# Two vision state-space layers on one core: output stages interleaved with the next batch's norm and projection, the second layer's preparation as a pipeline

## The chip, the core and the metric

The kernel runs on one core of one Trainium2 chip, as one program. The metric is the device time of one execution, in microseconds. The core has five engines that run side by side, each through its own queue in order: PE (TensorE, matmuls and transposes; it accumulates in PSUM), DVE (VectorE), ACT (ScalarE), POOL (GpSimd) and SP, which issues most of the DMA transfers. A few DMAs, the accumulating ones, are issued by POOL. PE's clock is throttled, and the profile shows what share of it was granted.

## The reference

Input x has 4 batches of 64 x 64 positions with 192 channels, float32. Two layers follow. The first is a selective scan in four directions. Cut to what matters (`xs` are the four orders of the positions; a group norm stands ahead of the projection and a residual is added behind):

```python
xz = jnp.einsum('bhwc,ec->bhwe', x, in_proj_weight)
xin, z = jnp.split(xz, 2, axis=-1)            # 384 inner channels each
xs = four orders of xin                       # rows, columns, both reversed
x_dbl = jnp.einsum('bkdl,kcd->bkcl', xs, x_proj_weight)
dts, Bs, Cs = split(x_dbl)                    # 12 + 16 + 16 rows
delta = softplus(dts @ dt_projs_weight + bias)
h = exp(delta * A) * h + delta * B * u        # along 4096 positions, 16 states
y_k = sum_n(h * C) + u * D
y = sum of the four directions, in place
out = (layernorm(y) * silu(z)) @ out_proj_weight.T
```

The second layer has the same outline. It has a 3 x 3 depthwise convolution with silu ahead of the scan, and its scan divides by a decay that falls below 1e-12 after few positions:

```python
decay = jnp.exp(jnp.cumsum(dt * A, axis=1))
h = decay * jnp.cumsum(dB_u / (decay + 1e-12), axis=1)
y = einsum(h, C) + u * D
```

## The kernel before, in words

A block is 512 positions (`LC`), so a batch has 8 (`NCH`); the 384 inner channels are 3 groups of 128 partitions (`ND`). A block in the layout "positions on partitions" is 4 tiles of 128 positions (`NJ`).

**First layer** (`FirstLayer.run`, once for each batch, one after the other):
- `norm` loads the 8 blocks of x (`xl`, three buffers), transposes them on PE into `xT`, takes statistics on DVE, and folds the result into the weights `w_in` and a bias, through a chain of small operations with a Sqrt on ACT.
- `project` (L500 on) runs over the 8 blocks: 6 matmuls to `pp`, evacuated by ACT to `u` (L522); 12 transposes to `q` (L529), copied by ACT to `ut` (L532) and multiplied by the sum of the D weights on DVE to `du` (L533). One DMA each stores `ut` and `du` (768 KB) to DRAM, into `uT` and into `y`, which starts with the D term. 6 more matmuls (L540) make the rows of dt, B and C by rows and by columns.
- `scans` keeps all engines but SP in an order written out by hand. It adds its results to `y` in DRAM, and leaves the gate z there too. The change doesn't touch it, except that it is told which y to use.
- `finish` is the output stage. `start` loads all 8 blocks of y (`yt`) and of the gate (`zg`, with a Silu on ACT, L873), in turn, and takes the mean and variance of each position (L881, L882): for the first two blocks, then for the other six, with one Sqrt (L884) for each of the two groups. `gated` scales `yt` on ACT (L896), transposes it on PE (L901), evacuates on ACT (L904) and multiplies by the gate on DVE (L907). `out` does the matmuls to `op` (L917), adds the input `xl` (L920) and stores. `gated` of the next block is written ahead of `out` of this one.

All four batches share one `y` in DRAM. The pools of `finish` and `project` reuse the same on-chip memory and PSUM banks, and one stage opens them after the other has closed them.

**Second layer** (`SecondLayer`), where each stage runs over all four batches:
- `project`: norm, projection, convolution; it leaves the positions near the borders in `uc`. Each direction's scan starts at a border and dies out within 256 positions, so only these are scanned.
- `prepare` has 8 steps (4 batches, the main 128 positions of each direction and an extension). A step loads `uc`, makes the dt, B and C rows (`xd`), and computes softplus: Abs (L1167) and Exp (L1168) on ACT, four operations on POOL (L1171 to L1175) with a Ln on ACT (L1174) beside them. On DVE follow the sum (L1177) and the running sums (line 989, a helper), the test whether the scan really died out (L1203 to L1206), and the product with u (L1241). PE transposes that, ACT copies it (L1222), and everything goes to DRAM (`keep`).
- `scans` has 9 scan steps for a batch, 36 in all, in an order written out by hand for PE, ACT, DVE and POOL: 4 of the main chunk with one state each, 2 of half chunks with two states, one of the extension, 2 of quarter chunks with four states. In each, ACT makes a weight (`sg`) and a decay (`a`); for the quarter chunks POOL multiplies ahead (L1285) and ACT does one wide activation (L1291). PE transposes the input (L1337), DVE weighs it (L1344) and scans, POOL multiplies by C (`c_product`, L1360), and PE adds it, transposed, to the outputs two steps later (L1378). The outputs of an extension (`yte`) and of the rest of a batch (`ytm`) are added to y in DRAM by 6 accumulating DMAs each, which POOL issues in a row (`store`, L1412 and L1415).
- `finish` is inherited and runs over all 32 blocks; the statistics of the next batch are started at the fifth block of this one.

Outside the two `scans` the order on each engine is made by the framework's scheduler at build time, from the order in which the program is written and from when it thinks operands are ready. A tile's memory is given out again when its readers are done; the number of buffers of each pool sets how far a producer can run ahead.

## Time and profile before

| | us |
|---|---|
| median of 3 runs | 11277.36 |
| lowest and highest | 11272.01, 11278.86 |
| the profiled execution, its own time | 11280.24 |
| its span, first to last instruction | 11278.4 |

| busy in the span | us | share |
|---|---|---|
| PE | 9593.1 | 85% |
| DVE | 9659.2 | 86% |
| ACT | 9787.2 | 87% |
| POOL | 8583.8 | 76% |

The mean granted clock of PE was 0.932. The stages, read from the first and last start of their lines in the trace (us from the span's start):

| stage | from | to |
|---|---|---|
| first layer, batch 0: norm and projection, start-up | 0 | 187.7 |
| its scans | 187.7 | 2397 |
| its output stage | 2397 | 2484 |
| batch 1: norm | 2484 | 2518 |
| projection | 2518 | 2608 |
| start-up of the scans | 2608 | 2657 |
| ... the same for the batches 1 to 3; last output stage | 9801 | 9886 |
| second layer: norm, projection, convolution | 9893 | 10456 |
| preparation | 10454 | 10648 |
| scans, with their start-up | 10648 | 11015 |
| output stage | 11015 | 11271 |

How to read the profile's lines. In a line of groups or waits, `L1177` is a line of the kernel and `dt<-dp,e` is what is written from what. A wait line says which engine at which line waited for which engine and line: us in total, how often, and the longest. A timeline line begins with the start and the length in us; in brackets stands how long the engine was idle ahead of it and what ended that. In a table by stretches, each engine has its busy time and the number of its instructions; PEclk is the granted share of PE's clock, then the busy share of the DMA engines and GB/s. In the strips of 40 slices each digit is a busy share in tenths.

### The profile page before, as it was taken

How to read it: one execution, taken by the hardware profiler on the slowest of the kernel's cores; microseconds unless marked ns; L12 is line 12 of the kernel's file. 1: busy time of each engine (PE TensorE's matmuls, PEld its weight loads, DVE VectorE, ACT ScalarE, POOL GpSimd, SP SyncE). 2: the span in 40 equal slices, each digit the busy share in tenths (PEclk: the TensorE clock that was granted, in tenths of full speed). 3: DMA queues.
4: the chain of work that ended last, by engine and by line, in shares of the span. 5: the costliest groups of instructions: out<-in, count | busy, mean ns of one | idle time of the engine just before them, and what ended most of it. 6: DMA issues, size and time to landing. Idle time of an engine off the chain costs nothing. (4 is left out here: it accounts for less than half of the span.)

```text
span 11278.4 us, 171696 instructions
## 1 busy us (share of the span) xinstructions
PE 9593.1 (85%) x61449; PEld 7301.6 (65%) x61449; DVE 9659.2 (86%) x11524; ACT 9787.2 (87%) x16986; POOL 8583.8 (76%) x2776
## 2 busy tenths in 40 slices
PE   7998888878988888888988888879988888788667
PEld 4776666655776666656766666647766666655356
DVE  4999899976999899957999899939998999888465
ACT  5999999977999999958999999949999999856567
POOL 3999899945999899928999899909998999700360
PEclk8999999988999999988999999979999999989688
DMA  4333333444333333344333334343333333434448
GB/s 124 109 105 98 94 98 100 97 133 125 109 104 99 94 99 98 97 149 112 111 100 96 96 98 98 89 164 107 109 100 94 98 98 98 127 114 128 159 104 272
DMA packets 831026, 1269.85 MB, mean 113 GB/s; under 512 B 99002, under 2 KB 514631, under 8 KB 829652
## 3 DMA queue, kind: packets, MB, share of 16 engines
q1 hardware_dynamic: 825300, 1252.49, 39.6%
q0 software_dynamic: 4864, 6.29, 0.4%
q8 instruction: 488, 8.00, 0.3%
q14 instruction: 374, 3.06, 0.1%
HBM read 958.19 MB, written 300.42 MB: 112 GB/s over the span
## 5 line engine op out<-in xcount | busy, mean ns | idle before, releaser
L738 POOL TENSOR_TENSOR h<-h,bct 128x1536 f32<-128x1536 f32 x2048 | 7062.4, 3469 | 591.4 <-DVE carry L734 487.9
L724 DVE TENSOR_TENSOR_SCAN h<-a,carry,x 128x512 f32<-128x512 f32 x5376 | 6607.0, 1267 | 238.7 <-PE x L716 191.7
L716 PE MATMUL x<-ident,xT 128*128 128x128 f32 x24576 | 4002.0, 287 | 817.7 <-DVE h L724 715.7
L699 ACT ACTIVATE xT<-dtuT,bT 128x384 f32<-128x384 f32 x8192 | 4358.6, 609 | 94.8 <-PE x L716 90.1
L716 PEld LDWEIGHTS x<-ident,xT 128*128 128x128 f32 x24576 | 2805.6, 145 | 2142.7 <-DVE h L724 925.7
L711 ACT ACTIVATE a<-dt,A_log_f 128x512 f32<-128x512 f32 x6144 | 3977.5, 716 | 0.0
L751 PE MATMUL yp<-ident,h 128*128 128x128 f32 x24576 | 3705.5, 277 | 9.2 <-POOL h L738 9.2
L751 PEld LDWEIGHTS yp<-ident,h 128*128 128x128 f32 x24576 | 2946.5, 144 | 78.8 <-issue 64.1
L615 PE MATMUL dp<-xd,w_dtb_f 13*128 13x512 f32 x1536 | 886.9, 661 | 213.6 <-DVE dt L644 212.0
L724 DVE TENSOR_TENSOR_SCAN h<-a,x 128x512 f32<-128x512 f32 x768 | 899.1, 1207 | 190.0 <-PE x L716 115.7
L628 POOL TENSOR_SCALAR wl<-e 128x1536 f32<-128x1536 f32 x128 | 189.1, 1478 | 919.6 <-ACT e L624 919.6
L490 PE MATMUL pp<-xT,w_in 96*128 96x512 f32 x1152 | 535.3, 615 | 0.0
L615 PEld LDWEIGHTS dp<-xd,w_dtb_f 13*128 13x128 f32 x1536 | 237.3, 190 | 457.0 <-DVE dt L644 341.2
L745 PE MATMUL yp<-yold,ident 128*128 128x512 f32 x768 | 444.1, 663 | 73.4 <-DMA yold<-y 73.4
L621 ACT ACTIVATE e<-dp 128x512 f32<-128x512 f32 x384 | 224.8, 585 | 311.9 <-DVE dt L644 161.7
L1106 DVE SCALAR_TENSOR_TENSOR acc<-pad,conv_w_s,acc 128x2048 f32<-128x2048 f32 x192 | 439.3, 2341 | 50.0 <-ACT acc L1104 49.4
L641 POOL TENSOR_TENSOR e<-e,wl 128x1536 f32<-128x1536 f32 x128 | 444.8, 3475 | 0.3
L1087 POOL MEMSET pad<- 128x66 f32 x12 | 1.9, 159 | 581.1 <-DVE acc L1106 456.0
L638 POOL TENSOR_TENSOR e<-e,dt 128x1536 f32<-128x1536 f32 x128 | 442.5, 3457 | 0.3
L490 PEld LDWEIGHTS pp<-xT,w_in 96*128 96x128 f32 x1152 | 221.5, 198 | 252.6 <-issue 243.5
L734 DVE TENSOR_REDUCE carry<-h 128x3 f32<-128x3 f32 x2048 | 322.7, 158 | 70.5
L644 DVE SCALAR_TENSOR_TENSOR dt<-dp,e 128x512 f32<-128x512 f32 x384 | 255.6, 666 | 74.6 <-POOL e L641 68.1
(172 smaller groups left out, 6855.1 us busy)
## 6 DMA issues: line engine op xcount, KB each, us to landing
bct<-xp SPq DMA_DIRECT2D x1024, 512.0 KB, 4.9
uT<-uT SPq DMA_DIRECT2D x64, 768.0 KB, 4.8
yold<-y SPq DMA_DIRECT2D x64, 768.0 KB, 7.9
y<-yt SPq DMA_DIRECT2D x64, 768.0 KB, 4.5
uT<-uT SPq DMA_DIRECT2D x128, 384.0 KB, 5.0
yold<-y SPq DMA_DIRECT2D x128, 384.0 KB, 5.4
y<-yt SPq DMA_DIRECT2D x128, 384.0 KB, 4.6
yt<-y SPq DMA_DIRECT2D x64, 768.0 KB, 10.8
```

Of the source, the lines that this page charges most:

```text
L490: self.tc.nc.tensor.matmul(pp, self.w_in[:, i, e * 128 : (e + 1) * 128], self.xT[:, i, t * LC : (t + 1) * LC], start=(i == 0), stop=(i == ...
L615: nc.tensor.matmul(self.dp[d], w, self.xd[0 : DR + 1, :], start=True, stop=True)
L638: nc.gpsimd.tensor_tensor(self.e, self.e, self.dt, ALU.subtract)
L641: nc.gpsimd.tensor_tensor(self.e, self.e, self.wl, ALU.add)
L699: nc.scalar.mul(xTs[g][:, j, :], it.dtuT[:, j * DI : (j + 1) * DI], it.bT[:, j, n : n + 1])
L711: nc.scalar.activation(as_[g][:, d, :], it.dt[:, d, :], AF.Exp, scale=scale)
L716: nc.tensor.transpose(xs[g, d][:, j * 128 : (j + 1) * 128], xTs[g][:, j, d * 128 : (d + 1) * 128], ident)
L724: nc.vector.tensor_tensor_scan(along(hs[g][:, d, :], it.k), along(as_[g][:, d, :], it.k), along(xs.pop((g, d)), it.k), 0.0 if it.first els ...
L738: nc.gpsimd.tensor_tensor(hs[g], hs[g], bc(cs[g - n % 2][:, n % 2, :], 1, ND), ALU.mult)
L745: nc.tensor.matmul(it.yp[b], ident, yo, start=True, stop=False, skip_group_check=True)
L751: nc.tensor.matmul(it.yp[b][:, i * 128 : (i + 1) * 128], hs[g][:, d, j * 128 : (j + 1) * 128], ident, start=False, stop=n == NS - 1, is_tr ...
L1106: nc.vector.scalar_tensor_tensor(acc, part(tap), weight(tap), acc, ALU.mult, ALU.add)
```

## The change

In the first layer, `run` now takes all batches. Between the scans of one batch and those of the next it calls `between`, which takes turns: one step of the output stage of the batch that is done, one step of norm and projection of the next. Both have become generators that yield after each block. To let them run at once, each batch has its own y, and the pools are open together, with fewer buffers and PSUM banks for each. The sum of the D weights is made once, at the start. `ut` and `du` are now one tile of 128 positions each, with three buffers, and are stored by four DMAs of 192 KB for a block where there was one of 768 KB. In the output stage, of both layers, the gate is loaded and put through Silu two blocks ahead of its use, no longer with y for a whole batch; the second layer has 14 buffers for y where it had 10, and 4 for the gate where it had 10.

In the second layer's preparation the part up to POOL's last operation is a function `start`, which is written one step ahead of the rest, with three buffers for what it makes. In the scans, the accumulating stores are put on a list and issued one at a time, behind the second and third scan of a step, two for each step; and weight and decay of a quarter chunk are made two steps ahead, with four buffers.

The diff, with the lines of `finish` and `project` that are only moved or indented left out:

```diff
@@ FirstLayer
+        self.dsum = wp.tile([128, DI], F32, name="dsum_f")
+        with tc.tile_pool(name="d4", bufs=1) as pd:
+            d4 = pd.tile([128, KD, DI], F32, name="d4")
+            nc.sync.dma_start(d4, w["D_rows"].partition_broadcast(128))
+            nc.vector.tensor_add(self.dsum, d4[:, 0, :], d4[:, 1, :])
...
-    def run(self, src, dst):
+    def run(self, srcs, dsts):
...
-            self.project(src)
-            self.scans()
-        self.finish([(src, dst, self.y_dram, self.gate)])
+            for b in range(len(srcs) + 1):
+                self.between([(srcs[b - 1], dsts[b - 1], self.ys[b - 1], self.gate)] if b else [], srcs[b : b + 1], b)
+                if b < len(srcs):
+                    self.y_dram = self.ys[b]
+                    self.scans()
+
+    def between(self, done, todo, b):
...
+            if done:
+                sbuf = pool("fy", 8), pool("fz", 3), pool("fl", 2), pool("fs", 1), pool("fw", 2)
+                banks = (2, 2) if todo else (4, 4)
+                steps.append(self.finish_steps(done, sbuf, (psum("fm", banks[0]), psum("fo", banks[1])), pool("fc", 1)))
+            if todo:
+                banks = (2, 2) if done else (3, 4)
+                pm, pt = psum("pm", banks[0]), psum("pt", banks[1])
+                steps.append(self.project_steps(todo[0], self.ys[b], pool("ld", 2 if done else 3), pool("st", 1), pm, pt))
+            while steps:
+                for g in list(steps):
+                    if next(g, None) is None:
+                        steps.remove(g)
...
-    def project(self, src):
-            pl, ps = pool("ld", 3), pool("st", 1)
-            pm = pool("pm", 3, space=bass.MemoryType.PSUM)
-            pt = pool("pt", 2, space=bass.MemoryType.PSUM)
-            pq = pool("pq", 2, space=bass.MemoryType.PSUM)
...
+    def project_steps(self, src, y, pl, ps, pm, pt):
+        self.norm(src, pl, ps, pt)
+        yield True
...
+            for j in range(NJ):
+                q = pt.tile([128, DI], F32, name="q", tag="tp")
...
+                ut = pl.tile([128, DI], F32, name="ut", bufs=3)
+                nc.scalar.copy(ut, q)
+                du = pl.tile([128, DI], F32, name="du", bufs=3)
+                nc.vector.tensor_mul(du, q, self.dsum)
+                at = slice(t * LC + j * 128, t * LC + (j + 1) * 128)
+                nc.sync.dma_start(self.uT_dram[at, :], ut)
+                nc.sync.dma_start(y[at, :], du)
...
@@ finish
-            py, pz, pl, ps, pw = pool("fy", 10), pool("fz", 10), pool("fl", 3), pool("fs", 2), pool("fw", 3)
+            sbuf = pool("fy", 14), pool("fz", 4), pool("fl", 3), pool("fs", 2), pool("fw", 3)
...
+        def load_gate(gate, t):
+            zg = pz.tile([128, ND, LC], F32, name="zg")
+            nc.sync.dma_start(zg, gate[t])
+            nc.scalar.activation(zg, zg, AF.Silu)
+            return zg
...
+        zgs = [load_gate(batches[b][3], t) for b, t in flat[:2]]
+        ready = {0: start(batches[0][2])}
+        yield True
+        v = gated(zgs.pop(0), *ready[0][0])
+        for i, (b, t) in enumerate(flat):
+            if i + 2 < len(flat):
+                b2, t2 = flat[i + 2]
+                zgs.append(load_gate(batches[b2][3], t2))
...
+            out(batches[b][0], batches[b][1], t, v)
+            v = more
+            yield True

@@ SecondLayer.prepare
+            def start(uc_dram, r):
+                uc = p3.tile([128, ND, LC], F32, name="uc")
+                nc.sync.dma_start(uc, uc_dram[:, r])
...
+                return uc, xd, e, dt
...
+            order = [(b, r) for b in range(len(batches)) for r in range(2)]
+            ready = [start(ucs[b], r) for b, r in order[:1]]
+            for i, (b, r) in enumerate(order):
+                if i + 1 < len(order):
+                    ready.append(start(ucs[order[i + 1][0]], order[i + 1][1]))
+                uc, xd, e, dt = ready.pop(0)
+                for d in range(ND):
+                    nc.vector.scalar_tensor_tensor(dt[:, d, :], dt_rows(xd, d), 0.0, e[:, d, :], ALU.max, ALU.add)
+                before = cum = sums(dt, before if r else None)
+                nc.vector.tensor_mul(e, dt, uc)
+                test(cum, r)
...
@@ SecondLayer.scans
-                sg[g] = p3.tile([128, ND, LC], F32, name="sg")
+                sg[g] = p4.tile([128, ND, LC], F32, name="sg")
...
-                as_[g] = p3.tile([128, ND, LC], F32, name="a")
+                as_[g] = p4.tile([128, ND, LC], F32, name="a")
...
-                store(y, b, 0)
+                stores.extend(store(y, b, 0))
...
+            def store_next():
+                to, of = stores.pop(0)
+                nc.gpsimd.dma_start(to, of, accum_op=ALU.add)
...
-                    if g + 1 < N:
-                        weight(g + 1)
-                        decay(g + 1)
+                    for q in (g + 1, g + 2):
+
+                        if q < N and (q - g == 2) == (len(flat[q][1]) == 4):
+                            weight(q)
+                            decay(q)
...
+                        if d > 0 and stores:
+                            store_next()
...
+                while stores:
+                    store_next()
...
@@ two_layer_vmamba
-    y = dr.tile([L, DI], F32, name="y")
+    ys = [dr.tile([L, DI], F32, name=f"y{b}") for b in range(NB)]
```

## The prediction

> **What bounds the kernel now.** I read the page's slices first. DVE and POOL are near nine tenths in four long plateaus and drop together between them.
>
> ```profile
> DVE  4999899976999899957999899939998999888465
> ...
> POOL 3999899945999899928999899909998999700360
> ```
>
> The same four drops are in both rows. I then asked the first and last start of each source line for the limits of the stages, and for the busy time of the engines in each:
>
> ```profile
> core 0: us, PE busy (x) PEld busy (x) DVE busy (x) ACT busy (x) POOL busy (x), PEclk, DMA share, GB/s
> ...
> 2397.00:2484.00 87.00, 52.10 (x294) 47.52 (x295) 42.69 (x109) 54.37 (x71) 0.00 (x0) 0.74 0.70 242
> 2484.00:2518.00 34.00, 24.93 (x93) 16.94 (x92) 15.04 (x29) 10.78 (x18) 0.00 (x0) 0.53 0.31 96
> 2518.00:2608.00 90.00, 90.00 (x280) 44.39 (x279) 28.96 (x45) 29.85 (x56) 0.00 (x0) 0.99 0.40 143
> ...
> 10453.00:10648.00 195.00, 131.81 (x304) 56.24 (x304) 73.45 (x193) 84.12 (x109) 79.43 (x32) 0.63 0.41 146
> ...
> 10662.00:11015.00 353.00, 233.46 (x1560) 192.64 (x1560) 212.81 (x364) 227.67 (x392) 211.84 (x132) 0.83 0.48 112
> 11015.00:11278.00 263.00, 196.93 (x1153) 181.18 (x1153) 167.29 (x435) 211.71 (x281) 0.26 (x1) 0.82 0.83 284
> ```
>
> The plateaus are the first layer's scans, four times 2204 us (first scan 187.7, last scan ended 2391.0, and so on). The change doesn't touch them, so 8816 us stay. Between two of them lie the output stage of one batch (2397 to 2484, no engine over 63%), the norm of the next (34 us, mostly DMA latency and a chain of small operations), its projection (90 us, PE without a gap at clock 0.99), and 49 us of start-up. In the second layer no engine is busy over 68% in the preparation or the scans. Chains set the time there. The waits name them, first those of the preparation (us, times, longest):
>
> ```profile
> DVE dt L1177 <- POOL e L1175: 69.5, 8, 13.6
> ...
> ACT e L1167 <- PE dp L1160: 35.8, 21, 8.4
> ```
>
> then those of the second scans:
>
> ```profile
> ACT sg L1291 <- POOL sg L1285: 54.7, 8, 13.4
> ...
> POOL y L1415 <- DMA y<-yte: 24.7, 7, 4.8
> ```
>
> What POOL does there is seen in its timeline (start, length): six accumulating stores in a row, each new place waiting until the one before has landed, and behind them three products by C (L1360) that had piled up.
>
> ```profile
> 10734.08 1.06 POOL L1412 DMA_DIRECT2D y<-yte  x1 [4.89 <-ACT yte L1396]
> 10738.52 1.70 POOL L1415 DMA_DIRECT2D y<-yte  x2 [3.38 <-DMA y<-yte]
> 10742.75 0.90 POOL L1412 DMA_DIRECT2D y<-yte  x1 [2.54 <-ACT xT L1326]
> 10746.67 1.68 POOL L1415 DMA_DIRECT2D y<-yte  x2 [3.02 <-DMA y<-yte]
> 10747.79 10.78 POOL L1360 TENSOR_TENSOR h<-h,bct 128x1536 f32<-128x1536 f32 x3
> ```
>
> **The sum** is made against the profiled execution's own 11280.2 us (span 11278.4). It lies 2.9 us above the median of the runs, 11277.4, and I take that off at the end.
>
> **1. Output stage beside norm and projection, three times.** Nothing is computed less; what is saved is idle time of PE. In the steady part of the output stage one block of 512 positions takes 5.2 us, in which PE issues 24 matmuls of 0.163 us and 12 transposes of 0.109 us: PE-bound. One projection block takes 11.6 us (24 matmuls 0.427 us apart, 12 transposes): PE-bound too. Interleaved they take PE 8 x (5.2 + 11.6) = 134 us; only starts can be hidden. From the end of a scan stage (2397) the norm needs nothing of the scans. Alone it took 34 us to the first evacuation of a projection (2484 to 2518). Now it has two load buffers for three, and shares the DMA engines with eight y blocks and two gates, 7.9 MB, 24 us at the 324 to 335 GB/s of the last stage's first 60 us. I put its end 50 us after the scans, 2447. By then PE has done two output blocks (they need the statistics of the first two y blocks only, as now at 2419). So 2447 + 93 of projection + 6 x 5.2 = 2571, and 9 us for stalls on two PSUM banks per use instead of three or four: 2580 against 2608, 28 us saved. Bounds: nothing, if the starts aren't hidden; 57, if five more blocks' worth of PE work fits into the norm (45 + 93 + 3 x 5.2 = 154 for 211). Three times: **-84**. ACT (54 + 30 + 11 = 95 us) and DVE (87) fit under PE's 165.
>
> What else is issued: ut and du leave as four stores of 192 KB per block instead of one of 768 KB, 48 more DMAs per batch at 0.37 us of SP's queue, 18 us in 165, and they stand ahead of xh, of the next xl, of ot and of the gate two blocks on. A store waits there for its copy on ACT or DVE, so the loads behind it are late by that; two blocks (34 us) of lead cover it. The next L522 would wait otherwise. ut and du have three buffers: four stores per block, each held until it lands (uT<-ut 3.8 us, y<-du 5.3 us), is 4/3 x 5.3 = 7 us of a 16.8 us block: covered.
>
> Here a rule speaks against the change. The Trainium skill, DMA: Bandwidth & Descriptors, section Bandwidth, asks for transfers of 1 MiB or more, and its section on the anatomy of a DMA prices one (issued from GpSimd; these go by SP) at 2.0 us plus its bytes by 436 GB/s. By that, as an estimate, four of 192 KB cost 9.8 us where one of 768 KB costs 3.8; for two tensors, eight blocks and four batches that would be +384 us if nothing overlapped. The sum would then end at about 11,450.
>
> The trace's rows say that they overlap: the second layer's y<-du of 256 KB land in 2.7 us and are issued 0.4 to 1 us apart. I price the split at nothing.
>
> The load of D (one DMA, three adds of 0.54 us) moves from each batch to the start: it lay in the norm's idle time; nothing, and 1.6 us per batch if that cover were gone. One y per batch only lets the next projection write while the last y is read; no instruction.
>
> **2. The first layer's last output stage** (9798 to 9886). Gates are loaded two ahead, so the eight y blocks come first: the second statistics (Sqrt of L884 at 9845.0, 37 us after the first y load) come at about 27. But the Silus, 6 x 1.48 us, that filled ACT's wait now stand in the steady part: 6.6 us of ACT per block, not 5.2. Net **-3** (bounds +5, -15).
>
> **3. Preparation as a pipeline.** POOL's chains (L1175) started at 10481.4 for the first and 10632.9 for the last of eight steps: 21.6 us apart on the mean, for 9.9 us of POOL. Until now a step's start was written behind the end of the one before; now one start is ahead. What is left per step: POOL 9.9 us; ACT 84/8 = 10.5; DVE 9.2; PE 131.8/8 = 16.5 at clock 0.63, or 12.5 at the 0.83 of the second scans, where PE is as busy. If ACT takes the start after next only behind this step's copies (12 us after POOL's end, and 8 us from there to the next Exp), two steps take 30. I take 13.5, between 12.5 and 15: 7 x (21.6 - 13.5) = **-57** (bounds -11 at 20 us, -82 at POOL's 9.9). The transfers (uc, dt, cum, dtuT, 3 MB per step, each landing in 3 to 5 us) lie beside it. Late next: PE.
>
> **4. Second layer's scans.** POOL per batch: 9 products of 3.47 us (31), 12 preparations of quarter chunks (13), two groups of stores, each 18.6 us from the end of the last product to the next (10729.2 to 10747.8): 81 us, which is the distance between batches (82 to 85). So POOL is the bound, by its queue. Two stores per step instead of six at once: of the waits, that for yte goes, and of three landings one falls under a product. Left per group 2 x 3.4 us of waiting and 4.5 of issue: 11.5. What queues behind a waiting store is one product (and at one step a quarter's preparation); its reader, the transposed add on PE, comes two steps of 5.9 us later, so a delay of 4 is hidden. Seven groups of 7 us (the very last group stays at the end), and 6 more for the last yte group, behind which the last product of all stood (17.6 us after the one before it): **-55** (bounds -20, if each place still waits; -92, if DVE and ACT at 58 per batch become the bound). The quarter chunks' weights one step earlier, with four buffers, take most of ACT's 54.7 us of waiting; that is inside these 55, as ACT isn't the bound.
>
> **5. The last output stage** (11015 to 11278). Between 11075 and 11215 the slices of 20 us move 264 to 377 GB/s and ACT is busy for 17.7 to 19.9 of them; PE waited 29 us at the start. y first: second statistics at about 11044 for 11056.5; 14 y buffers for 10 let a batch's y come together. ACT's remaining 196 us from 11044 and 7 of output would give 11247 for 11271; at each batch's statistics I leave some 4 us of stall: **-13** (bounds +10, because the Silus lose their cover; -24).
>
> Sum: -84 - 3 - 57 - 55 - 13 = -212; 11280.2 - 212 - 2.9 = **11065 us**.
>
> **Rivals.**
> *The starts are not hidden* (13 in 100). y's landing (2397 to 2404.6) and the eight y loads ahead of xl in SP's one queue keep the norm back until the output blocks are half done. For it: SP issued the y loads in 0.4 to 4 us each with the queue full. Against: xl of the output stage was issued at 2394.8, before the y stores. Part 1 gives nothing: 11149.
> *Preparation stays a chain* (8): PE remains cold and a step takes 20 us; part 3 gives 11: 11111.
> *All parts reach an engine's floor* (12): the lower bounds, -171 - 15 - 82 - 92 - 24, would be 10893; half way to them from my forecast is 10979.
> *Slower: the split stores* (9). If ut and du land late, three buffers bind: a block takes 4/3 of the landing. Under the output stage's load the y and gate loads landed in 10.8 and 11.4 us; that would give 15.2 us, still under 16.8. Binding begins at 12.6 us of landing; at 19.4 a block takes 25.9, 9.1 more, and 8 x 9.1 x 3 = 218 eats all. At twice today's, 22.8 us: 30.4 per block, +326, 11391. Against it: stores land in 2 to 5 us wherever they run now, and the mix asks for 217 GB/s where 330 is reached.
>
> **Numbers.** The forecast as it stands has 58 in 100, by itself 11,000 to 11,130. The range 10,960 to 11,165 takes in the first two rivals and part of the floors; outside are the slower case and the rest of the floors. A measurement of this kernel tells about 0.2% (23 us) from no change. Faster 0.89, the same 0.02, slower 0.09.
>
> **What would show it.** Distance from a batch's last scan to the next batch's first: 266 us now (2391.0 to 2657.3), 238 if right, with PE's granted clock over 0.85 in it; in the preparation L1175 13.5 us apart; in the second scans no POOL gap over 5 us between stores and batches 67 us apart; in the last stage the second Sqrt before 11,045 by today's clock. Wrong would make it: gaps of PE on yt or zg in the middle of the mix, q or ut waiting on a store, L1167 still waiting on PE, a first-layer scan stage other than 2204 us (1% of it is 88 us).

## The result, and the profile after

The changed kernel takes 11106.25 us (median of four, 11104.26 to 11106.99); the kernel before, run beside it, takes 11278.11. The ratio is 0.9848, with a 95% interval of 0.9831 to 0.9865: 172 us less. The forecast was 11065, with 10960 to 11165 as its range. The profiled execution took 11106.54 us, its span 11104.6.

Stage by stage the picture is less kind to the forecast. The limits are the first and last instructions of each stage in the two traces.

| stage, us | before | after | difference | forecast |
|---|---|---|---|---|
| start to the first scan | 187.7 | 184.2 | -3.5 | 0 |
| first layer's four scan stages | 8805.3 | 8793.0 | -12.3 | 0 |
| the three gaps between them | 266.3, 267.2, 268.4 | 231.3, 225.5, 228.2 | -116.9 | -84 |
| first layer's last output stage | 91.6 | 86.3 | -5.3 | -3 |
| second layer's projection | 566.9 | 569.4 | +2.5 | 0 |
| preparation, to the second layer's first scan | 215.0 | 228.3 | **+13.3** | **-57** |
| second layer's scans | 312.1 | 271.9 | -40.2 | -55 in these two |
| from the last scan to the first statistics | 42.6 | 50.5 | +7.9 | |
| last output stage | 248.1 | 228.1 | -20.0 | -13 |

The preparation, which was to win 57 us, lost 13. The gaps won a third more than I said. The profile's slices of the changed kernel look much as before. At the right end, in the slices 38 and 39 that hold the preparation and the second scans, DVE has risen from 4 and 6 to 6 and 7, and POOL only from 3 and 6 to 3 and 7.

```profile
DVE  4999899976999899968999899949998999878675
...
POOL 3999899955999899938999899929998999700370
```

The windows of the changed kernel (length, busy time and count of each engine, PE's granted clock, DMA share, GB/s): the first gap before and after 2447 us, where the forecast put the norm's end, the preparation, the second scans, the last stage.

```profile
2391.00:2447.00 56.00, 30.69 (x156) 24.47 (x157) 35.01 (x95) 35.64 (x51) 0.00 (x0) 0.70 0.86 294
2447.00:2577.00 130.00, 128.83 (x511) 77.75 (x510) 49.83 (x88) 58.18 (x95) 0.00 (x0) 0.97 0.48 168
...
10340.00:10530.00 190.00, 119.07 (x268) 52.56 (x266) 122.86 (x192) 80.22 (x97) 83.75 (x32) 0.62 0.34 125
...
10546.00:10869.00 323.00, 225.18 (x1546) 184.54 (x1544) 211.92 (x364) 229.12 (x387) 212.74 (x132) 0.83 0.54 131
10869.00:11097.00 228.00, 195.48 (x1153) 179.55 (x1153) 163.42 (x433) 197.99 (x271) 0.00 (x0) 0.90 0.91 306
```

In the gap PE has no hole from 2447 on (128.8 us busy of 130, at clock 0.97): projection and output blocks are one stream of PE work, as the change intends. In the preparation DVE is busy for 122.9 us, where it had 73.5 in the 195 us window of before, with the same 192 or 193 instructions. That is the first thing to explain: nothing was added for DVE, and it got 49 us more to do.

### The profile page after: what moved, and what is told of

Same layout as the page of the kernel before. It is cut to its first block, busy times and chain, and to the rows that moved or that the text cites. A ratio compares the mean times of both kernels' runs of the same rounds, so it can differ in the third digit from the quotient of the medians.

```text
span 11104.6 us, 172135 instructions
## 1 busy us (share of the span) xinstructions
PE 9551.9 (86%) x61449; PEld 7273.6 (66%) x61449; DVE 9693.3 (87%) x11515; ACT 9775.8 (88%) x16979; POOL 8587.9 (77%) x2776
## 5 line engine op out<-in xcount | busy, mean ns | idle before, releaser
L638 ACT ACTIVATE e<-dp 128x512 f32<-128x512 f32 x384 | 224.7, 585 | 269.3 <-DVE dt L661 155.4
```

## The experiments

Where no spread is given, a kernel was run once, with its profile. Single stages are compared, since a stage that no edit touches moves the whole by 10 us and more.

### The preparation: what took the gain

POOL's timeline of the changed kernel (start, length). L1213 ends the chain of a step; the forecast wanted these 13.5 us apart.

```profile
10356.45 3.43 POOL L1213 TENSOR_TENSOR e<-e,wl 128x1536 f32<-128x1536 f32 x1 [1.40 <-ACT wl L1212]
...
10369.71 4.97 POOL L1213 TENSOR_TENSOR e<-e,wl 128x1536 f32<-128x1536 f32 x1 [2.30 <-ACT wl L1212]
...
10381.27 3.42 POOL L1213 TENSOR_TENSOR e<-e,wl 128x1536 f32<-128x1536 f32 x1
10402.62 1.47 POOL L1209 TENSOR_SCALAR wl<-e 128x1536 f32<-128x1536 f32 x1 [17.93 <-ACT e L1206]
...
10405.73 3.68 POOL L1211 TENSOR_TENSOR e<-e,dt 128x1536 f32<-128x1536 f32 x1
10409.49 3.68 POOL L1213 TENSOR_TENSOR e<-e,wl 128x1536 f32<-128x1536 f32 x1
10429.38 1.63 POOL L1209 TENSOR_SCALAR wl<-e 128x1536 f32<-128x1536 f32 x1 [16.21 <-DVE dt L1270]
```

The first three starts come 13.3 and 11.6 us apart. Then POOL stands idle for 12 to 18 us in every step, and the mean of all seven distances is 21.4, against 21.6 before. Two things in the trace could do it. One is the running sums on DVE (line 1020, the helper). Their rows in the changed kernel (ns: least, median, most):

```profile
L1020 DVE TENSOR_TENSOR_SCAN cum<-one,cum,dt x48: 447/454/3608, 10382.9 to 10519.6; 128x128 f32<-128x128 f32 x48
L1020 DVE TENSOR_TENSOR_SCAN cum<-keep_s,dt x24: 657/1594/3850, 10361.7 to 10507.0; 128x256 f32<-128x256 f32 x24
```

Before, the most was 476 and 680. The long ones have a pattern. Five sums in a row take 10 us together:

```profile
10404.87 10.01 DVE L1020 TENSOR_TENSOR_SCAN cum<-keep_s,dt 128x256 f32<-128x256 f32 x5
```

The second and third of them take 3.85 and 3.83 us; they begin beside L1211 and L1213 on POOL and end 0.55 us after each of these has ended. The first takes 1.31 us and ends 0.53 us after L1210, which has one input. A sum that would take 0.67 us seems to be held until POOL's operation is over, and then runs. The other candidate is the order on PE, in the waits of the changed kernel (us, times, longest):

```profile
PE tp L1257 <- DVE end L1239: 55.4, 6, 12.4
...
DVE dt L1270 <- PE dp L1191: 30.0, 9, 9.6
```

PE stands before the transposes of a step's storing part until DVE's product is done (the profile names the small operation behind it), and the dt matmuls of the next step are queued behind it. Four kernels separate the two.

**Undo the pipeline alone** (a step's start again behind the end of the one before; the buffers stay).

```diff
-            ready = [start(ucs[b], r) for b, r in order[:1]]
-            for i, (b, r) in enumerate(order):
-                if i + 1 < len(order):
-                    ready.append(start(ucs[order[i + 1][0]], order[i + 1][1]))
-                uc, xd, e, dt = ready.pop(0)
+            for b, r in order:
+                uc, xd, e, dt = start(ucs[b], r)
```

> The changed kernel with one thing undone: in the preparation a step's start is again written directly ahead of its own rest. In the changed kernel the eight chains of POOL lie 21.5 us apart on the mean (10356.4 to 10506.6) where they lay 21.6 apart before, and the running sums of DVE take 1875 and 801 ns where they took 666 and 458. Two theories. Port: the running sums (two SBUF inputs) and POOL's two-input operations can't run at once, and the pipeline put them side by side. Order: on PE the transposes of a step stand ahead of the next step's dt matmuls and wait for DVE's product, so that the next step's Abs, Exp and POOL chain can't start before this step's sums are done. Both expect here: sums back to 666 and 458 ns, chains 21 to 22 us apart, and from the last convolution operation to the first scan about 215 us as before instead of 228; 11093 us in all. If it stays at 228, it was the other edits of the preparation (three buffers, product ahead of the test).

Measured: 11094.3 us; the preparation 234.6, the chains 22.6 apart. The running sums are quick again, all of them:

```profile
L1020 DVE TENSOR_TENSOR_SCAN cum<-one,cum,dt x48: 454/461/476, 10369.8 to 10511.4; 128x128 f32<-128x128 f32 x48
L1020 DVE TENSOR_TENSOR_SCAN cum<-keep_s,dt x24: 665/666/681, 10348.8 to 10486.7; 128x256 f32<-128x256 f32 x24
```

So it is the company of POOL that slows them, and the pipeline as written is worth 6 us in its stage. The whole is 12 us shorter here only because the first layer's scans took 16 us less in this run, which has nothing to do with the edit. The stage does not come back to 215, and 13 of the 20 us are seen: POOL's first L1213 comes 40.7 us after the last instruction of the convolution, 38.5 in the changed kernel, 28.0 before. The first load of `uc` is issued 9 us behind the projection's last store, in both; before it was 11 us ahead of it. With the order undone this remains, so it comes with the other edits of the stage. The other 7 us are the seven distances (22.6 for 21.6); what lengthened them was not tried.

**The mask of the running sums in PSUM.** The first operand of the sums (`self.keep`, or a broadcast one) is copied once into PSUM, so that the operation has one input from SBUF. Another buffer of the transposes pays for it.

```diff
-            ps_t = pool("pst", 3, space=bass.MemoryType.PSUM)
+            ps_t = pool("pst", 2, space=bass.MemoryType.PSUM)
+            mask = pool("psk", 1, space=bass.MemoryType.PSUM).tile([128, LC], F32, name="mask")
+            nc.vector.tensor_copy(mask, self.keep)
...
-                            scan_add(nc, cum[:, d, part], self.keep[:, part], dt[:, d, part], 0.0, k == 1)
+                            scan_add(nc, cum[:, d, part], mask[:, part], dt[:, d, part], 0.0, k == 1)
...
-                            one = self.one.to_broadcast([128, SEG])
+                            one = mask[:, SEG + 2 : 2 * SEG + 2]
```

> The changed kernel with the mask (and the ones) of the running sums in a PSUM bank, taken from the transposes' three; so a running sum has one SBUF input. Port: the sums go back to about 0.67 and 0.46 us beside POOL, DVE loses 46 us of busy time in the preparation, and the stage gains 30 to 45: 11060 to 11075. If the port isn't the cause the sums stay at 1.9 and 0.8 us. Order: the sums may be short, but each step still waits for the transposes of the one before; 20 us or more per step, the stage gains under 15: 11090 or more.

Measured: 11057.4 us, 49 below the changed kernel; the preparation 190.3, which is 38 of the 49; the chains 15.9 us apart. The pipeline is as it was, POOL works beside DVE as before, and the sums are quick:

```profile
L1020 DVE TENSOR_TENSOR_SCAN cum<-mask,cum,dt x48: 457/458/483, 10374.4 to 10478.7; 128x128 f32<-128x128 f32 x48
L1020 DVE TENSOR_TENSOR_SCAN cum<-mask,dt x24: 661/665/691, 10361.1 to 10465.3; 128x256 f32<-128x256 f32 x24
```

This settles the first candidate: in these runs the sums are slow when both inputs lie in SBUF and POOL has an operation running, and only then. The Trainium skill has such a rule, in SBUF — State Buffer, section "SBUF: two separate sides": DVE with two SBUF inputs and a GpSimd operation that reads SBUF take one pair of ports by an exclusive lock, and the loser waits for the whole instruction. The runs agree: 0.67 us becomes 3.85, beside an operation of 3.68.

The collision is not gone, though; it has moved to what still has two inputs in SBUF. DVE's product takes 2.50 us in the median where it took 1.72, and POOL's L1215, the same operation as L1213 above, 4.8 us in seven of its eight steps where it takes 3.42 alone.

```profile
L1274 DVE TENSOR_TENSOR e<-dt,uc x8: 1733/2498/3097, 10364.6 to 10479.1; 128x1536 f32<-128x1536 f32 x8
...
10397.33 4.85 POOL L1215 TENSOR_TENSOR e<-e,wl 128x1536 f32<-128x1536 f32 x1
```

**The storing part later** (the function `keep` of a step, written behind the start of the step after next, with four buffers for what it reads).

```diff
...
+            done = []
             for i, (b, r) in enumerate(order):
                 if i + 1 < len(order):
                     ready.append(start(ucs[order[i + 1][0]], order[i + 1][1]))
+                if done:
+                    keep(*done.pop())
...
-                keep(batches[b][r], xd, dt, cum, e)
+                done.append((batches[b][r], xd, dt, cum, e))
+            keep(*done.pop())
```

> The changed kernel with a step's transposes, copies and stores written one step later, behind the start of the step after next (with four buffers for what they read). The mask stays in SBUF. Order: PE no longer waits for the product with the next dt matmuls behind it; steps of 14 to 17 us, the stage gains 35 to 55: 11050 to 11070. Port alone: the sums stay slow or get slower, since more of POOL lies beside them; DVE's 15.4 us per step is the floor, and if POOL and DVE take turns (9.9 + 9.6 us and more) 20 us: gain under 15, 11090 or more.

Measured: 11084.4 us; the preparation 209.0, the chains 19.4 apart, with sums as slow as before the edit (1892 and 781 ns on the mean). That lies between what the two theories asked for. Of the 19 us in the stage, 15 are the seven distances and 6 the first chain, which comes 32.6 us after the convolution for 38.5; 1 is lost behind the last chain. The first `uc` is again loaded 11 us ahead of the projection's last store. Only the sizes of the pools differ there, so I take it for a matter of which memory the tile gets; that was argued, not tried by itself.

**Both.**

> Both edits together. If both causes hold, steps of 12.5 to 14 us, as the prediction had it (PE at a clock of 0.7 to 0.83): chains of POOL over 88 to 98 us instead of 150, the stage gains 50 to 65: 11040 to 11055. If only one holds, no better than the better one of the single edits.

Measured: 11057.2 us, the preparation 187.7, the chains 16.4 apart. With quick sums the order on PE gives nothing more: the first chain comes 8 us sooner, and the distances and what follows the last chain take 6 of them back.

What holds the remaining 16 us is PE for the most part. Between the first and the last chain it is busy for 98.1 of 111 us in the kernel with the mask (first row), and for 106.5 of 117 in the kernel with both, profiled in its later run (second row); DVE has 79 and 76. In the changed kernel PE had 98 of 151 us between them, and DVE 108.

```profile
10356.00:10467.00 111.00, 98.08 (x212) 38.70 (x212) 79.20 (x154) 63.94 (x77) 75.65 (x29) 0.64 0.45 168
...
10348.00:10465.00 117.00, 106.52 (x211) 40.36 (x210) 76.25 (x152) 59.96 (x73) 68.48 (x28) 0.59 0.42 158
```

The granted clock is the column behind POOL: it stays between 0.57 and 0.63 from 10350 to 10500 in all of these kernels. Why it stays low with PE this busy is not shown here.

### The gaps: is it the interleaving?

**Output stage, then norm and projection, written one behind the other**, with all other edits kept (y first, stores split in four, one y per batch). Each stage has the buffers and banks that it gets when it is alone.

```diff
-                self.between([(srcs[b - 1], dsts[b - 1], self.ys[b - 1], self.gate)] if b else [], srcs[b : b + 1], b)
+                if b:
+                    self.between([(srcs[b - 1], dsts[b - 1], self.ys[b - 1], self.gate)], [], b)
+                if b < len(srcs):
+                    self.between([], srcs[b : b + 1], b)
```

> The changed kernel with the interleaving of the first layer undone, all else kept: output stage, then norm and projection, each with the pools that it has when it is alone. From a batch's last scan to the next one's first it was 266.3, 267.2 and 268.4 us before and is 231.3, 225.5 and 228.2. Interleaving (PE's idle starts are hidden, and the start-up of the scans begins 9 us earlier): 250 to 266 again, three times 25 to 38 more; 11180 to 11220. The other edits (four stores per block, gate two blocks ahead, D made once, one y per batch): it stays within 15 us of 228; 11110 to 11150. If a store of 192 KB cost as much more as its size says, two tensors, eight blocks, then the projection alone, with nothing beside it, would be up to 96 us longer per batch: over 11300. The first layer's scans, 12 us shorter in all since the change: if the earlier start-up is the reason they go back to 2200 to 2203 each.

Measured: 11200.8 us; the gaps 259.7, 263.8 and 261.0, so 99 of the 117 us are gone. DVE's timeline of this kernel, the end of the first scan stage and the start of the next:

```profile
2381.59 0.16 DVE L754 TENSOR_REDUCE carry<-h 128x3 f32<-128x3 f32 x1
...
2641.29 3.44 DVE L744 TENSOR_TENSOR_SCAN h<-a,x 128x512 f32<-128x512 f32 x3 [12.25 <-ACT a L731]
```

The interleaving is the cause. With the split stores but no interleaving the gaps are 3 to 7 us shorter than before. That does not make the split free. Output stage and norm are 12 to 15 us shorter in this kernel, and the projection, from its first evacuation to its last copy, is longer: 93.8, 98.5 and 95.7 us for 90.3, 91.6 and 90.4. ACT waits there 16.2, 18.7 and 9.4 us in the three gaps for a store of `ut` to land and free one of the three buffers; the slowest took 9.6 us. The first gap:

```profile
L550 ACT COPY ut<-q x32: 479/482/497, 2500.0 to 2587.0; 128x384 f32<-128x384 f32 x32
...
  DMA uT<-ut: 16.2, 8
```

How much of the 3 to 7 us in the projection is the split's was not tried by itself. In the changed kernel, with output blocks in between, the profile puts at most 0.3 us of ACT's waiting in a gap down to such a landing, and 3.5 of DVE's. The store (192 KB, 32 of them for `ut`) lands there in half the time of one of 768 KB before (3.8 us in the median):

```profile
L551 SPq DMA_DIRECT2D uT<-ut x32: 319/383/1831, 2467.0 to 2578.6; - x32
...
DMA to landing us min/median/max: 1.8/1.9/3.8
```

One thing in the gap I had not priced. Before, the scans' first load of `xd` was issued at 2617.5, 9 us behind the projection's last copy; the eight stores `xp<-xw` stood ahead of it in SP's queue (the last at 2616.8). In the changed kernel it is issued 24 us ahead of the last copy, and those stores come behind it (from 2580.1):

```profile
L617 SPq DMA_DIRECT2D xd<-xp x4: 451/488/582, 2553.0 to 2655.2; - x4
```

From the projection's last copy to the next first scan it is now 39.8, 37.3 and 37.5 us in the three gaps, for 48.9, 50.7 and 51.1. In the serial kernel the load comes 11 us behind the copy and behind those stores again, and the three are 53.8, 52.1 and 51.9. So that, too, comes with the interleaving. Why the load came late before (its place in the queue, or memory that it shares with the projection) was not tried by itself.

### The second layer's scans: two edits, one gain

The timeline of POOL in the changed kernel shows the split stores at work. Each store of two (or one) stands between two products, and up to the last batch's no group of six is left.

```profile
10641.16 0.83 POOL L1455 DMA_DIRECT2D y<-ytm  x1 [4.23 <-DVE h L1020]
10641.73 3.73 POOL L1392 TENSOR_TENSOR h<-h,bct 128x1536 f32<-128x1536 f32 x1
10645.11 1.17 POOL L1455 DMA_DIRECT2D y<-ytm  x1
10649.76 0.87 POOL L1455 DMA_DIRECT2D y<-ytm  x1 [3.47 <-DMA y<-ytm]
10650.34 3.74 POOL L1392 TENSOR_TENSOR h<-h,bct 128x1536 f32<-128x1536 f32 x1
```

Batches are 62 to 73 us apart (forecast 67, before 77 to 85). Three times POOL still idles longer ahead of a store than the 5 us of the forecast (5.2, 7.5 and 5.4). The waits of the changed kernel in this stage:

```profile
ACT sg L1323 <- POOL sg L1317: 37.0, 7, 10.6
...
POOL y L1455 <- DMA y<-yte: 21.4, 5, 7.3
...
PEld yp L1410 <- POOL h L1392: 15.2, 8, 4.7
```

**Stores in a row again**, the quarter chunks' weights still two steps ahead.

```diff
-                    stores.extend(store(it.y, flat[g][2], SEG))
+                    store_all(store(it.y, flat[g][2], SEG))
...
-                stores.extend(store(y, b, 0))
+                store_all(store(y, b, 0))
...
+            def store_all(r):
+                for to, of in r:
+                    nc.gpsimd.dma_start(to, of, accum_op=ALU.add)
```

> The changed kernel with the accumulating stores of the second layer's scans issued six in a row again; the earlier weights of the quarter chunks stay. The scans gained 40 us to the last scan and lost 8 behind it. Stores as the cause of both: scans 300 to 312 us again, and the tail from last scan to the first statistics back to 43 from 50.5; 11130 to 11140. Weights as the cause: scans stay under 285, 11100 to 11115.

Measured: 11121.8 us, the scans 301.8, the tail from the last scan to the first statistics 48.0, where 43 was expected (more on that below). PE waits for POOL's products again, as it did before (55.7):

```profile
PEld yp L1410 <- POOL h L1392: 53.0, 8, 8.5
```

**The quarter chunks' weights one step ahead**, the stores still split.

```diff
-                        if q < N and (q - g == 2) == (len(flat[q][1]) == 4):
+                        if q < N and q - g == 1:
```

> The changed kernel with weight and decay of the quarter chunks made one step ahead again, as all others; stores stay spread. My prediction held that this part is worth nothing by itself, since ACT is not the bound: scans 272 to 278 us, 11104 to 11112. If the quarter chunks' wait on POOL is a bound of its own (it is 37 us now, 54.7 before), the scans lose 15 to 30: 11120 to 11135.

Measured: 11137.0 us, the scans 297.4. Now ACT waits for POOL's preparation, and DVE behind it for ACT (16.6 us in the changed kernel):

```profile
ACT sg L1323 <- POOL sg L1317: 61.5, 8, 16.7
...
DVE x L1376 <- ACT sg L1323: 42.7, 8, 14.9
```

**Both undone.**

> The changed kernel with both parts of the second layer's scans undone: the stores in a row, and the quarter chunks' weights one step ahead. One alone cost 30 us, the other 25.5, of 40 gained. If these two edits hold the whole gain and each is needed for most of it, the scans take 312 again, as before, and the whole about 11,146. If the two simply add, 327 and 11,162. If a third thing (the step's copies, the fourth buffer) gave part of the gain, 300 and 11,134.

Measured: 11143.4 us, the scans 312.9, so the 312.1 of before are back and no third part shows. The four values make a table: nothing 312.1 or 312.9, the weights alone 301.8, the split stores alone 297.4, both 271.9 (266 to 273 in the other kernels that carry both, with the steps in this order). Alone they win 10 and 15 us, together 40. Each takes away a wait that the other had left to decide: a chain that waits for POOL at two places is as long as the later of them.

### The tail and the last stage

**Ten y buffers instead of fourteen** in the last output stage.

```diff
-            sbuf = pool("fy", 14), pool("fz", 4), pool("fl", 3), pool("fs", 2), pool("fw", 3)
+            sbuf = pool("fy", 10), pool("fz", 4), pool("fl", 3), pool("fs", 2), pool("fw", 3)
```

> The changed kernel with 10 instead of 14 buffers for y in the second layer's output stage. That stage takes 228 us from first statistics to last output, 248 before. If the buffers carry the gain, 238 to 248 again: 11115 to 11126. If the order of the loads does (y first, gates two blocks ahead), 228 to 233: 11105 to 11110.

Measured: 11097.2 us; the last stage 228.1, with fourteen 228.1. The buffers have no part in it (the other kernels, with fourteen, have 222 to 229). What is left is the order of the loads (y first, gates two ahead), which was not undone by itself. Measured against the first statistics, the second Sqrt begins 23.5 us later, before 33.3:

```profile
10892.18 0.32 ACT L903 ACTIVATE rs<-mv,ln_eps_s 128x24 f32<-128x24 f32 x1
```

ACT also changes its function tables less often, since a batch's Silus and Sqrts alternate less. The groups of such loads in the changed kernel's last stage:

```profile
L915 ACT ACT_TABLE_LOAD x6 | 7.7, 1283 | 4.7 <-DMA zg<-gate 4.6
L903 ACT ACT_TABLE_LOAD x5 | 6.4, 1283 | 0.1
```

Before there were 9 and 8 of them: six fewer, 7.7 us of ACT (four of the 32 Silus are missing from this trace, so a load may be too; the kernel with ten buffers, whose trace has all 32, has twelve loads).

The tail, from the last scan to the first statistics, lost 8 us. Before, `yte`'s six stores of the last batch stood ahead of the last product (first row); in the changed kernel all twelve stand behind it.

```profile
10990.91 4.00 POOL L1360 TENSOR_TENSOR h<-h,bct 128x1536 f32<-128x1536 f32 x1
...
10818.38 3.42 POOL L1392 TENSOR_TENSOR h<-h,bct 128x1536 f32<-128x1536 f32 x1 [0.17 <-POOL h L1392]
10821.74 0.90 POOL L1455 DMA_DIRECT2D y<-yte  x1
...
10847.77 0.90 POOL L1455 DMA_DIRECT2D y<-ytm  x1 [6.82 <-DMA y<-yte]
...
10860.21 1.67 POOL L1455 DMA_DIRECT2D y<-ytm  x2 [2.96 <-DMA y<-ytm]
```

That order is not shown to be the cause. With the stores in a row again, `yte`'s six are ahead of the last product as before, and the tail is 48.0 us; with both parts undone it is 47.0. The kernels that have the changed order lie between 46.7 and 50.6. Single stores of the tail land late in most of them (up to 7.6 us behind their issue in the changed kernel, 5.0 before); in the one with ten y buffers none takes over 4.8, and its tail is the 46.7. So late landings may be some 4 of the 8 us, and the rest stays open.

**The extension step before the half steps**, on top of the mask in PSUM, so that `yte` is ready two steps sooner.

```diff
-                steps = [(main, (n,)) for n in range(4)] + [(half, (n, n + 1)) for n in (4, 6)] + [(ext, (0,))]
+                steps = [(main, (n,)) for n in range(4)] + [(ext, (0,))] + [(half, (n, n + 1)) for n in (4, 6)]
```

> The mask of the running sums in PSUM, as before, and the second layer's extension step taken ahead of the two half steps of its batch. Theory: the 50.5 us from the last scan to the last stage's first statistics hold two groups of stores one behind the other (yte, then ytm), because the extension is only two steps from the end; taken earlier, its stores leave between the products of the half and quarter steps, and some 21 us of the tail go (yte's first store to ytm's first, 26 us, less the 5 that ytm's copies need behind the last product). Whole kernel 11057 - 20 = 11037, scans unchanged at 267. Rival 1: the tail is the last product and ytm's way, the yte stores fill a gap: tail 48 to 50, 11057. Rival 2: the moved step makes two light steps meet and POOL's products pile up behind the stores: scans 10 us longer per batch, 11075 or more.

Measured: 11071.1 us (median of four), 0.9813 of before (0.9796 to 0.9829). The tail is 43.1 us for 49.8, and the scans 279.5 for 267.1. So the theory had the place right and a third of the size: the stores do leave between the products, but only four of the six are ahead of the last product, and the last two are then waited for.

```profile
10802.05 3.75 POOL L1394 TENSOR_TENSOR h<-h,bct 128x1536 f32<-128x1536 f32 x1
10805.46 2.02 POOL L1457 DMA_DIRECT2D y<-yte  x2
10814.28 0.89 POOL L1457 DMA_DIRECT2D y<-ytm  x1 [6.80 <-DMA y<-yte]
...
10829.03 1.68 POOL L1457 DMA_DIRECT2D y<-ytm  x2 [2.69 <-DMA y<-ytm]
```

The second rival, longer scans, took more than the tail gave, at 12 us in all instead of 10 per batch. `ytm`'s own six stores and the wait ahead of them (6.8) are now the tail.

**The same with the storing part later.**

> The kernel with the mask in PSUM and the early extension step, and the storing part of a preparation step written behind the next step's start. If PE's order costs nothing once the running sums are quick, within 5 us of the same kernel without the late storing part; if it still holds the chain, 10 to 19 less (the 19 that it gave with slow sums).

Measured: 11056.7 us, 14 below the median of the kernel above, so the whole time falls where it was expected if PE's order still held the chain. The stages don't bear that out. The preparation has 186.2 for 194.8, and of these 8.6 us 6 are the first chain (32.6 us after the convolution for 38.4) and 2.5 the seven distances. The tail is 43.3 and the scans 277.9, and the first layer's scans, which no edit touches, are 6 us shorter.

### The version to keep

**The mask in PSUM and the storing part later**, timed five times.

> The kernel with the mask in PSUM and the storing part of a preparation step written behind the next step's start, timed in rounds: 11,057 in its one look, with the preparation at 188 us, and the early extension step left out since it gave back in the scans what it took from the tail. If that look was typical, 0.980 of the kernel before and some 49 us below the changed one; if one look is worth no more than the 5 us by which a stage of the first layer's scans varies from kernel to kernel, anything from 11,045 to 11,070.

Measured: 11054.6 us (median of five, 11047.15 to 11062.35), 0.9798 of the kernel before (0.9785 to 0.9812). Its interval lies below that of the changed kernel. It beats both, by 228 us and by some 52. The preparation takes 188.8 us in it, the second scans 269.3. Against the same kernel without the moved extension step the early step gains nothing: 11056.7 in its one run lies inside this spread.

## Why the prediction was right or wrong

The time was in the range, 41 us above the forecast. It got there by errors that partly cancel: preparation 70 us worse than said, scans and tail of the second layer 23 worse, gaps 33 better, the last stage 7 better, and 16 in stages that I held fixed.

1. **Gaps: right, and too small.** Counted from the end of the scans, the projection's last copy comes after 191.5, 188.2 and 190.7 us, before 217: 27 less, where the forecast said 28. Inside, two errors cancel, and that is luck. The first evacuation of the projection comes 74, 72 and 73 us after the scans, where 2447 meant 56; from there it takes 117, 116 and 117 us, where the forecast had 133, since three output blocks were done by then and not two, and the 9 us for stalls on two PSUM banks did not come. PE as the only limit in the second half is what the trace has. (By the rows that it shows, PE's 165 us are 167; nothing hangs on it.) The term that failed is the "49 us of start-up", which the forecast left as it was. It is 38 on the mean now, since the first load of the scans no longer stands behind the projection. That is 12 us three times, 36; the 3 that the projection's end gave less than forecast come off, and it is the 33.

2. **The split stores: right in the mix.** The slower rival wanted 19.4 us of landing there; the median is 1.9 to 2.1, the longest 4.1, and ACT hardly waits for one. The estimate of +384 us from the page's price, which was for stores that don't overlap, didn't come true. But three buffers do bind where the projection stands alone: the serial kernel shows ACT waiting 9 to 19 us a batch, with landings of up to 9.6 us. That the split costs nothing holds for the interleaved kernel.

3. **Preparation: wrong.** The step that failed is "What is left per step: ... DVE 9.2". That was DVE's time when POOL and DVE took turns. The pipeline's purpose is to let them work at once, and at once DVE needs 15.4 (122.9 / 8). No row of before shows the two side by side, so that cost wanted a bound from both sides and got none. A second step failed with it: the 12.5 us for PE took the clock of the second scans, 0.83, and the clock stayed at 0.62, where PE's own 119 us are 14.9 a step. "The transfers ... lie beside it. Late next: PE" was wrong on what is late next while the sums are slow: DVE is, and PE waits for it. With quick sums PE is late next, as said, and the step is 15.9; that this is near the 15 that I gave for ACT's order as the worse case is chance. Of the 70 us, 56 are the seven distances, 10 the first chain, which comes later because `uc` is loaded later, and 4 lie behind the last chain.

The rival "Preparation stays a chain" gave 11111, and 21.4 us a step is what it said in substance. But its cause was a cold PE, one at a low clock. PE did stay at 0.62, but with the mask in PSUM the step falls to 15.9 at the same clock, so that was not the reason for 21.4. And the time would have come out higher had the gaps not won more. That it lies near 11106 speaks for its step time, not for its reason.

4. **Second scans: the mechanism right, the split of the gain wrong.** The stores spread over the steps, POOL without groups of six up to the last batch, batches 69 us apart on the mean for the 67 forecast: as said, but for three gaps of POOL of 5.2 to 7.5 us. But "that is inside these 55, as ACT isn't the bound" dismissed the half that was needed: with the stores alone the scans win 15, not 49. ACT is not the bound by its busy time, and still its wait for POOL's preparation was the next link of the chain. And "6 more for the last yte group, behind which the last product of all stood" was wrong in sign: the product no longer stands behind the stores, but all the stores now stand behind the product, and the tail is 8 us longer, not 6 shorter. What makes it longer stays open, as shown above.

5. **The last stage: right in mechanism.** The second Sqrt was to come 12.5 us earlier, counted from the start of the stage; it comes 10 earlier, counted from the first statistics. "14 y buffers for 10 let a batch's y come together" was wrong; ten give the same. Five or six table loads fewer, up to 7.7 us of ACT, are about the 7 us that the sum lacked; that they are the reason was not tried.

**Not explained:** the first layer's scans, which no edit touches, were 12 us shorter than in the profile of before. In all the changed kernels together they range from 8777 to 8799, in a profile each, and before it is 8805 in a single profile (the prediction's four times 2204, 8816, is a misreading: the four take 2203, 2201, 2201 and 2200). The earlier start-up is not the cause: in the serial kernel, where it is undone, they take 8792. It is 0.14% in the changed kernel, and I have no cause.

## What to carry to other kernels

Before you put two engines side by side, look whether their durations were measured alone: a row from a stage in which they took turns says nothing about the stage in which they don't, least of all for DVE with two SBUF operands beside POOL. If one operand is a constant, a copy of it in PSUM takes that operation out of the collision; then look which operation is left in it, and which engine is next. And when a chain waits for one engine at two places, price the two edits as a pair, by undoing each and both; an edit that wins a quarter of the gain alone may be needed for most of it.

## What the runs showed of the hardware

- A running sum on DVE with both inputs in SBUF (128x256) takes 0.67 us alone, up to 3.85 beside an operation with two inputs on POOL (3.68 us), and 1.31 where it waited for the end of one with a single input (L1210). It goes from 0.46 to 3.61 at 128x128. With one of the inputs in PSUM both stay at their own time (most: 691 and 483 ns) with the same POOL work beside them.
- POOL pays too: its last operation of the chain takes 4.97 us instead of 3.42 at 10369.71, while a DVE product with two SBUF inputs is running. With the mask in PSUM that is so in seven of eight steps (4.82 to 4.85 us).
- Stores of 192 KB land in 1.9 us in the median in the changed kernel's gap, where those of 768 KB took 3.8. In the serial kernel, whose projection stands alone, the slowest took 9.6, and ACT waited for them.
- In the preparation PE was busy for 88% and 91% of the time between the first and the last chain at a granted clock of 0.64 and 0.59 (mask, and both), and in the second scans of the changed kernel for 70% at 0.83.
